# Turning normalised tiles by DMA, as two 16-bit planes, in the memory attention of a six-block kernel

## The chip, the cores and the metric

The kernel runs on one core of a Trainium2 chip. The metric is the device time of one execution in microseconds (us); the kernel before took 2589.55 us, the median of 3 runs (2587.43 to 2590.55). Work is spread over TensorE (PE in the profile), VectorE (DVE), ScalarE (ACT), GpSimd (POOL), and transfers whose instructions are queued on SyncE (SP).

## The reference

The program runs six residual blocks over eight sequences of 1024 tokens with 256 features, all in fp32: an FP4 feed-forward, a decaying linear attention, the same FP4 feed-forward, a ternary feed-forward, a memory attention, and the ternary feed-forward again. The change lies in the memory attention. Cut to what matters, that block is:

```python
x = layernorm(x)
q, k, v = x @ wq.T, x @ wk.T, x @ wv.T          # 16 heads of 16
sq, sk = elu(q) + 1, elu(k) + 1
out_m = sq @ memories[m] / (sq . memory_norms[m])     # 4 memories
mem_out = sum over m of softmax_m(mean of sq . memory_norms[m]) * out_m
local = (sq @ cumsum(sk v^T)) / (sq . cumsum(sk))     # causal linear attention
x = x + (g * mem_out + (1 - g) * local) @ w_o.T
```

## The kernel before

The 8192 tokens are 64 tiles of 128 tokens, held on the 128 partitions, and 16 groups of 4 tiles; a sequence is 2 groups. TensorE contracts over partitions, so each normalised tile, tokens by features, has to be turned to features by tokens before it can be multiplied by the projection weights. The turned group is the tile `xt`, 2 halves of 128 features by 512 tokens.

The block is `attn_memory`. A prelude at step 0 normalises, turns and projects groups 0 to 2. Then a loop runs 64 steps and 5 more that drain it; step i works on tile i, which is tile j = i mod 4 of its group, and on older tiles in later stages. A group is projected (line 2003: q or k, 512 tokens at a time, one half of the features a step) in the steps j = 3, 0, 1, 2, two to three groups ahead of its own attention. Tile keys and values come from `keys` (line 1745), which reads `xt` again at the group's own steps. In each step:

- TensorE computes scores (`sc`, line 1263), products with the memories (`pmo`, 1786), the weighted values (`py`, 1329 and 1347), the transpose `psd` (1929), in a step with j = 3 the divisors (`pr`, 1667), the transposes `pyt` and `pn` (1969, 1973), a projection (`pk` or `pq`, 1361), the output product `po`, in a step with j = 2 the turning of a group, and the keys and values `pkv` (1754, 1361).
- VectorE first runs the batch statistics of later tiles that are due in that step (`ln.advance(i, 0)`, line 1951), then the reciprocal `rw` (1955), `y` (1981), two of the four score weightings (`at`, 1272), the layer-norm terms that are due (`ln.advance(i, 1)`, line 1998), the last `at`, the output addition (2014), the elu (1627), and the weightings of the next step's memory products (1799). In every second step a running sum (1646) stands ahead of the statistics.
- ScalarE copies results out of PSUM (`nt` 1914, `yt` 1976, `vz` 1763, `kd` 1770), computes `ee` (1622, 1623), masks queries (`qz`, 1774) and normalises groups (`norm`, two instructions a tile, lines 317 and 325).
- GpSimd adds the memories (1902), adds `y` (1989), the state (1944), the clamps (1680) and the products by the running sum (1636).

`norm(t + 1)` is written in a step with j = 1, `norm_turn(t + 1, (3, 0))` in the next one, with t = i // 4 + 2. `norm_turn` makes eight 128x128 transposes on TensorE into two PSUM banks and copies each bank to `xt` on ScalarE. There is one buffer for the normalised group `xn`, and four for `xt`.

Two things set the order. Whatever goes through `pin` (all of TensorE and VectorE here) keeps the order of the program text. ScalarE and GpSimd are not pinned in this block: the framework's planner places their instructions, the earliest in the text first among those that it takes to be ready, so an instruction far down in the text can be moved forward into a gap. SP has nothing queued in this block.

The statistics of later groups are spread over the steps by `PLANS["memory"]`: sizes of the shares in groups, and for each the step by which it is due. A share has a statistics entry for each tile (`bn_stats` and `bn_aggr`, lines 235 and 236) and four entries of layer-norm terms at its end (a seed of three instructions, lines 248 to 255, and three Newton steps of three, lines 262 to 264), all on VectorE.

Of the kernel before, what the change touches and what calls it, by code (L numbers as in the profile page):

```python
# [9 lines left out]
F32 = mybir.dt.float32  # L10
F32R = mybir.dt.float32r
BF16 = mybir.dt.bfloat16
I32 = mybir.dt.int32
AF = mybir.ActivationFunctionType
ALU = mybir.AluOpType
AX = mybir.AxisListType
# [2 lines left out]
P = 128  # L19
D = 256  # L20
# [3 lines left out]
G = 4  # L24
TG = G * P
# [14 lines left out]
def macaron_kernel(  # L40
# [25 lines left out]
    nc = tc.nc  # L66
    NB, S, _ = x.shape
    NG = NB * S // TG
    GB = S // TG
# [60 lines left out]
    for g in range(NG):  # L130
        xg = xpool.tile([P, G, D], F32, name=f"x_{g}")
        X.append(xg)
        if g == 0:
# [4 lines left out]
                out=A0.lng[:, H : H + 2], in_=gamma_rep.rearrange("(m p) -> p m", p=P)  # L138
# [23 lines left out]
    for m in range(NM):  # L162
        nc.sync.dma_start(
            out=mem_d[:, :, m, :],
            in_=memories[m].rearrange("h d e -> (h d) e").rearrange("(c p) e -> p c e", p=P),
        )
        nc.sync.dma_start(
            out=nrm_d[:, :, m],
            in_=memory_norms[m].rearrange("h d -> (h d)").rearrange("(c p) -> p c", p=P),
# [10 lines left out]
        out=tri, in_=ones, pattern=[[1, P]], compare_op=ALU.is_ge, fill=0.0, base=0,  # L180
# [5 lines left out]
        out=blk8, in_=ones[:, 0:HT], pattern=[[-HD, HT]], compare_op=ALU.is_ge, fill=0.0, base=0,  # L186
# [3 lines left out]
        out=blk8, in_=blk8, pattern=[[HD, HT]], compare_op=ALU.is_ge, fill=0.0, base=HD - 1,  # L190
# [47 lines left out]
    def norm_terms(mv, r, b):  # L238
# [8 lines left out]
        def seed():  # L247
# [3 lines left out]
                nc.vector.tensor_scalar(  # L251
                    r.bitcast(I32), va.bitcast(I32), -0.5, float(RSQRT_SEED), ALU.mult, ALU.add
                )
# [14 lines left out]
    def statistics(sizes, dues):  # L268
# [44 lines left out]
        def normalize(dst, g, only=None, pin=lambda ins: ins, apart=False):  # L313
            def centred(j):
                n = G * g + j
                pin(
                    nc.scalar.activation(
                        dst[:, j, :], X[g][:, j, :], AF.Identity, bias=lb[:, n : n + 1]
                    )
                )  # L320

            def scaled(j):
                n = G * g + j
                pin(
                    nc.scalar.activation(
                        dst[:, j, :], dst[:, j, :], AF.Copy, scale=lr[:, n : n + 1]
                    )
# [25 lines left out]
        "ternary": ((2, 2, 4, 4, 4), [max(0, g - 1) for g in range(NG)]),  # L353

        "memory": (
            (GB + 3, 3, 4, NG), [max(0, G * (g - GB) - 4) for g in range(NG)]
        ),
    }
    begun = {}
# [1 line left out]
    def begin(kind, left):  # L361

        if kind not in begun:
            ln = statistics(*PLANS[kind])
            begun[kind] = [ln, list(ln.first)]
        ln, shares = begun[kind]
        for _ in range(-(-len(shares) // left)):
            shares.pop(0)()
        if left == 1:
            xn = xn_pool.tile([P, G, D], F32, tag="xn", name="xn")  # L370
            ln.normalize(xn, 0)
            begun[kind] = (ln, xn)
# [16 lines left out]
    def fp4_round(v, sc, pool, mul, pin):  # L389
        vb = v.rearrange("p (b k) -> p b k", k=16)  # L390
        np_, nb, _ = vb.shape
        mg = pool.tile([P, nb * 16], F32, tag="q_mg", name="q_mg")[:np_]
        nc.scalar.activation(mg, v, AF.Abs, scale=FP4_MAGIC)

# [4 lines left out]
    def transpose_group(src, dst, psum, tag, both_act=False, pin=lambda ins: ins):  # L399

        for k in range(2):
            pt = psum.tile([P, TG], F32, tag=tag, name="pt")
            for j in range(G):
                pin(
                    nc.tensor.transpose(
                        pt[:, j * P : (j + 1) * P], src[:, j, k * P : (k + 1) * P], ident
                    )
                )
            if k == 0 or both_act:
                nc.scalar.copy(dst[:, k, :], pt)  # L410
            else:
                pin(nc.vector.tensor_copy(dst[:, k, :], pt))

    def fp4_first(xn, mg, pool):

        v = xn.rearrange("p t d -> p (t d)")
        vb = v.rearrange("p (b k) -> p b k", k=16)
        nb = G * D // 16
        wide = [P, nb, 16]
        am = pool.tile([P, nb], F32, tag="q0_am", name="q_am")  # L420
        pin(nc.vector.tensor_reduce(am, vb, AX.X, ALU.max, apply_absolute_value=True))
        sc = pool.tile([P, nb], F32, tag="q0_sc", name="q_sc")
        pin(nc.vector.tensor_scalar(sc, am, -1.0 / 6.0, -1e-12, ALU.mult, ALU.min))
        rs = pool.tile([P, nb], F32, tag="q0_rs", name="q_rs")
        pin(nc.vector.tensor_scalar(rs, sc, -FP4_TIE, None, ALU.mult))
        pin(nc.vector.reciprocal(rs, rs))
        nc.gpsimd.tensor_tensor(vb, vb, rs[:, :, None].to_broadcast(wide), ALU.mult)

        def magnitudes():
            nc.scalar.activation(mg, v, AF.Abs, scale=FP4_MAGIC)  # L430

        def round_it():
            for op in (ALU.add, ALU.subtract):
                pin(nc.vector.scalar_tensor_tensor(v, mg, FP4_LEAST, v, ALU.max, op))
            nc.gpsimd.tensor_tensor(vb, vb, sc[:, :, None].to_broadcast(wide), ALU.mult)

        return magnitudes, round_it
# [10 lines left out]
    with (  # L448
# [16 lines left out]
        def log_decays():  # L465
            pin(nc.scalar.activation(gsig, gsig, AF.Sigmoid))

            pin(nc.scalar.activation(ea, A0.lng, AF.Abs))
            pin(nc.scalar.activation(ea, ea, AF.Exp, scale=-1.0))
            pin(nc.scalar.activation(ea, ea, AF.Ln, bias=1.0))  # L470

        ii = prep_q.tile([P, P], I32, name="ii", bufs=1)
        df = prep_q.tile([P, P], F32, name="df", bufs=1)
        nc.gpsimd.iota(ii, pattern=[[1, P]], base=0, channel_multiplier=-1)
        nc.gpsimd.tensor_copy(df, ii)
        nc.gpsimd.tensor_scalar(df, df, 0.0, 1.0, ALU.max, ALU.mult)
        ii2 = prep_q.tile([P, P], I32, name="ii2", bufs=1)
        tf = prep_q.tile([P, P], F32, name="tf", bufs=1)
        nc.gpsimd.iota(ii2, pattern=[[1, P]], base=1, channel_multiplier=0)
        nc.gpsimd.tensor_copy(tf, ii2)  # L480
        ii3 = prep_q.tile([P, 1], I32, name="ii3", bufs=1)
        sf = prep_q.tile([P, 1], F32, name="sf", bufs=1)
# [107 lines left out]
        xn = xn_pool.tile([P, G, D], F32, tag="xn", name="xn")  # L590
# [776 lines left out]
    def attn_decay(after):  # L1367
        with ExitStack() as st:
# [18 lines left out]
            def norm_turn(g):  # L1387
                xt = lnp.tile([P, 2, TG], F32, tag="xt", name="xt")
                transpose_group(xns.pop(g), xt, ps_b, "pb", both_act=True, pin=pin)
                qz = lnp.tile([P, 2, 2, TG], F32, tag="qz", name="qz")  # L1390
                qg = lnp.tile([P, 2, TG], F32, tag="qg", name="qg")
                kt = lnp.tile([P, 2, TG], F32, tag="kt", name="kt")
                proj[g] = (xt, qz, qg, kt)
# [175 lines left out]
    def attn_memory(after):  # L1569
        with ExitStack() as st:  # L1570
            lnp = st.enter_context(tc.tile_pool(name="a1_ln", bufs=2))
            bp = st.enter_context(tc.tile_pool(name="a1_b", bufs=GB + 2))
# [4 lines left out]
            ps_s = st.enter_context(tc.tile_pool(name="a1_ps", bufs=4, space=PSUM))  # L1577

            ps_n = st.enter_context(tc.tile_pool(name="a1_pn", bufs=1, space=PSUM))
            xns, proj, sums, mix, state, chunk, ys = {}, {}, {}, {}, {}, {}, {}  # L1580
            ksum, carry = {}, {}
            vzs = spaced_values(vp)
# [4 lines left out]
            def bank(n, shape, name):  # L1587
                return ps_n.tile(shape, F32, tag=f"b{n}", name=name)

            def norm(g):  # L1590
                xn = xn_pool.tile([P, G, D], F32, tag="xn", name="xn")
                ln.normalize(xn, g)
                xns[g] = xn

            def norm_turn(g, banks, both_act=True):
                xt = bp.tile([P, 2, TG], F32, tag="xt", name="xt")
                xn = xns.pop(g)
                for k in range(2):
                    pt = bank(banks[k], [P, TG], "pt")
                    for j in range(G):  # L1600
                        pin(
                            nc.tensor.transpose(
                                pt[:, j * P : (j + 1) * P], xn[:, j, k * P : (k + 1) * P], ident
                            )
                        )
                    if k == 0 or both_act:
                        nc.scalar.copy(xt[:, k, :], pt)
                    else:
                        pin(nc.vector.tensor_copy(xt[:, k, :], pt))
                sq = bp.tile([P, 2, TG], F32, tag="sq", name="sq")  # L1610
                sk = bp.tile([P, 2, TG], F32, tag="sk", name="sk")
                proj[g] = (xt, sq, sk)
# [194 lines left out]
            n = NG * G  # L1807
            clamps, summed = [], None
            held = {}
            for i in range(n + 5):  # L1810
                a, b, c, d, e = i - 1, i - 2, i - 3, i - 4, i - 5
                g, j = divmod(i, G)
                t = g + GB
# [187 lines left out]
                if i < n and last < NG:  # L2001
                    m, of_q = (j + 1) % 4 // 2, j % 2 == 0
# [19 lines left out]
                weigh_one(0)  # L2022
                if added:
                    added()
                if i < n and j == 2 and t + 1 < NG:
                    norm_turn(t + 1, (3, 0))
                if i < n:
                    keys(i, 3 if elu else 2)
# [11 lines left out]
                    output()()  # L2040
                if i < n and i % CB == 0:
                    mixing[2]()
                if i < n and j == 1 and t + 1 < NG:
                    norm(t + 1)
                if n - 14 <= i < n - 2:
                    begin(after, n - 2 - i)

# [6 lines left out]
    f0_stack.close()  # L2054
    ffn_ternary(False, "memory")
    attn_memory("ternary")
    ffn_ternary(True)

# [47 lines left out]
```

## Time and profile before

| | |
|---|---|
| median of 3 runs | 2589.55 us |
| the profiled execution | 2594.43 us, of which the span from first to last instruction is 2592.7 |
| memory attention (first `pt` transpose to last `psd`) | 1749 to 2315 us |
| PE busy in it, 1990 to 2060 us | 69.48 of 70 us |
| DVE, ACT, POOL there | 60.95, 40.48, 39.12 of 70 us |
| transposes of `xn` (line 1602) in the block | 128, of which 104 in the loop |
| copies of them on ScalarE (line 1607) | 29, mean 588 ns |

A busy TensorE is not at its peak, since its instructions overlap and their ends are modelled; the chain of work that ended last tells better how much time each of them holds up the rest. A duration of an instruction in the groups (273 ns for a transpose) is longer than its share of the chain for the same reason. In the timeline, the bracket behind an instruction is the idle time of its engine before it and what ended it.

### The profile page before, as it was taken

The page shows a single profiled execution, that of the slowest core. Times are in us where ns is not written, and L with a number is a line of the kernel's source. Part 1 is how long each engine was busy: PE and PEld are TensorE (multiplying, and loading weights), DVE is VectorE, ACT ScalarE, POOL GpSimd, SP SyncE. Part 2 cuts the span into 40 slices and gives each one's busy share as a digit, 9 for nine tenths or more (in the row PEclk, how much of TensorE's full clock was granted, in tenths as well). Part 3 has the DMA queues.
Part 4 walks back from the last instruction along what each step waited for, and adds up shares of the span by engine and source line. Part 5 has one row for each costly group of instructions (what it writes and reads, how often), then busy time and mean ns, then how long its engine had stood idle before and what let it go on. Part 6 is the DMA issues. An engine that isn't in the chain of part 4 may idle for free.

```text
span 2592.7 us, 52415 instructions
## 1 busy us (share of the span) xinstructions
PE 2506.9 (97%) x20426; PEld 1868.6 (72%) x20426; DVE 2087.8 (81%) x4808; ACT 1235.1 (48%) x2785; POOL 900.9 (35%) x895
## 2 busy tenths in 40 slices
PE   4899999999999999999999999999999999999999
PEld 2577777766666666777777689995677776778998
DVE  7898888758878778988888599647888888879864
ACT  5344444334333333444444276656555555437664
POOL 4565555521101003555555300004555555530000
PEclk9899999999999999999999999999999999999999
DMA  7455556500000002556555300000000000000001
GB/s 218 87 117 115 113 118 116 107 23 18 10 22 14 2 2 48 114 116 115 117 116 113 66 1 1 1 1 1 2 2 2 2 2 2 2 2 26 33 33 41
DMA packets 199897, 132.40 MB, mean 51 GB/s; under 512 B 138048, under 2 KB 174944, under 8 KB 199648
## 3 DMA queue, kind: packets, MB, share of 16 engines
q1 hardware_dynamic: 198704, 127.85, 22.8%
q8 instruction: 161, 2.64, 0.4%
q0 software_dynamic: 240, 0.54, 0.1%
q14 instruction: 88, 0.72, 0.1%
q10 hardware_dynamic: 704, 0.66, 0.1%
HBM read 80.77 MB, written 16.52 MB: 38 GB/s over the span
## 4 chain that ended last, share of the span: by engine, by line
PE 84%; DVE 11%; ACT 2%; issue 1%; DMA 1%; POOL 1%; SPq 0%; DVEq 0%; POOLq 0%; ACTq 0%
PE po L960 11%; PE pu L861 10%; PE pg L861 10%; PE po L1220 9%; PE ph L1193 9%; PE sc L1263 5%; PE py L1347 5%; PE pq L1361 4%; PE pkv L1361 4%; PE po L1361 4%; PE pk L1361 4%; PE py L1329 2%; PE pmo L1786 2%; DVE at L1272 1%; DVE qp L804 1%
## 5 line engine op out<-in xcount | busy, mean ns | idle before, releaser
L960 PE MATMUL po<-wd,ht 128*128 128x256 f32 x1536 | 358.1, 383 | 0.6 <-DVE x L969 0.5
L861 PE MATMUL pu<-wgu,xt 128*128 128x352 f32 x1024 | 349.6, 464 | 8.3 <-DVE h L876 7.9
L861 PE MATMUL pg<-wgu,xt 128*128 128x352 f32 x1024 | 348.8, 463 | 4.4 <-ACT sg L871 4.1
L960 PEld LDWEIGHTS po<-wd,ht 128*128 128x128 f32 x1536 | 294.6, 193 | 62.4 <-issue 2.2
L871 ACT ACTIVATE sg<-pg 128x352 f32<-128x352 f32 x256 | 118.1, 461 | 451.5 <-PE pg L861 422.6
L817 POOL TENSOR_TENSOR h<-h,q_rs 128x704 f32<-128x704 f32 (+1 forms) x128 | 176.2, 1376 | 413.1 <-DVE q_rs L811 413.1
L861 PEld LDWEIGHTS pu<-wgu,xt 128*128 128x128 f32 x1024 | 186.5, 193 | 112.3 <-issue 19.6
L861 PEld LDWEIGHTS pg<-wgu,xt 128*128 128x128 f32 x1024 | 195.0, 191 | 97.8 <-ACT sg L871 9.2
L1220 PE MATMUL po<-w,hl 128*128 128x256 f32 x1024 | 243.7, 280 | 1.4 <-DVE hl L1204 1.2
L1220 PE MATMUL po<-w,hh 128*128 128x256 f32 x1024 | 243.3, 280 | 0.0
L1902 POOL TENSOR_TENSOR mo<-mo 128x256 f32<-128x256 f32 x192 | 164.2, 855 | 196.6 <-DVE mo L1799 188.1
L927 POOL TENSOR_TENSOR ht<-gt,ht 128x768 f32<-128x768 bf16 x124 | 205.7, 1659 | 0.0
L1193 PE MATMUL ph<-xh,w 128*128 128x512 f32 x512 | 204.4, 401 | 1.4 <-ACT hf L1201 0.6
L1193 PE MATMUL ph<-xl,w 128*128 128x512 f32 x512 | 201.8, 395 | 0.0
L1204 DVE TENSOR_TENSOR hl<-hf,hh 128x512 fp32r<-128x512 f32 x256 | 168.3, 684 | 39.4 <-ACT hh L1202 35.9
L1220 PEld LDWEIGHTS po<-w,hl 128*128 128x128 f32 x1024 | 192.1, 188 | 4.5 <-DVE hl L1204 2.5
L1220 PEld LDWEIGHTS po<-w,hh 128*128 128x128 f32 x1024 | 192.1, 188 | 2.6 <-DVE x L1228 0.3
L1201 ACT ACTIVATE hf<-ph,b1c 128x512 f32<-128x512 f32 x256 | 168.0, 695 | 18.5 <-PE ph L1193 16.1
L1272 DVE TENSOR_TENSOR at<-sc,dec 128x512 f32<-128x512 f32 x256 | 158.6, 682 | 11.8 <-PE sc L1263 11.8
L886 DVE SCALAR_TENSOR_TENSOR h<-qp,h 128x704 f32<-128x704 f32 x124 | 110.2, 889 | 69.1 <-ACT qp L821 68.9
L1272 DVE TENSOR_TENSOR at<-sc,tri 128x512 f32<-128x512 f32 x256 | 164.9, 679 | 0.4 <-PE sc L1263 0.4
L1202 ACT CAST hh<-hf 128x512 fp32r<-128x512 f32 x256 | 149.2, 628 | 17.0 <-PE po L1220 15.2
(276 smaller groups left out, 5303.0 us busy)
## 6 DMA issues: line engine op xcount, KB each, us to landing
ht<-sd SPq DMA_DIRECT2D x124, 384.0 KB
xt<-sd SPq DMA_DIRECT2D x56, 256.0 KB
sd<-sct SPq DMA_DIRECT2D x124, 64.0 KB
x<-in_x SPq DMA_DIRECT2D x15, 512.0 KB
out<-x SPq DMA_DIRECT2D x15, 512.0 KB
t_raw<-in_w_t SPq DMA_DIRECT2D x16, 256.0 KB
gt<-gd SPq DMA_TRANSPOSE x124
gtx<-xn SPq DMA_TRANSPOSE x56
```

The costliest lines, as they stand in the source:

```text
L817: pin(mul.tensor_tensor(vb, vb, rs[:, :, None].to_broadcast([P, nb, 16]), ALU.mult))
L861: nc.tensor.matmul(ps, lhsT=xts[g][:, 2 * j + k, :], rhs=wgu[:, k, (2 * q + of_up) * NHALF : (2 * q + of_up + 1) * NHALF], start=(k == 0), ...
L927: nc.gpsimd.tensor_tensor(wide.rearrange("p c t -> p (c t)"), grid.rearrange("p c t -> p (c t)"), wide.rearrange("p c t -> p (c t)"), ALU. ...
L960: nc.tensor.matmul(po, lhsT=ht[:kn, c, :], rhs=wd[:kn, c, :], start=(c == 0), stop=(c == NC - 1),)
L1193: nc.tensor.matmul(ph, lhsT=w1[:, k, f * P : (f + 1) * P], rhs=xt[:, k, :], start=(k == 0 and xt is xh), stop=(k == 1 and xt is xl),)
L1201: nc.scalar.activation(hf, ph, AF.Gelu, bias=b1c[:, f : f + 1])
L1202: nc.scalar.copy(hh[:, f, :], hf)
L1204: nc.vector.tensor_tensor(hl[:, f, :], hf, hh[:, f, :].bitcast(F32), ALU.subtract)
L1220: nc.tensor.matmul(po, lhsT=ht[:, f, j * P : (j + 1) * P], rhs=w2[:, f, :], start=(f == 0 and ht is hh), stop=(f == NF - 1 and ht is hl),)
L1272: nc.vector.tensor_tensor(at, sc.rearrange("p m (e t) -> p (m e) t", e=2), weight, ALU.mult)
L1361: nc.tensor.matmul(dst, lhsT=lhsT, rhs=rhs, start=n == 0, stop=n == len(parts) - 1)
L1902: summed = nc.gpsimd.tensor_tensor(mo[:, :, :, 0, :], mo[:, :, :, 0, :], mo[:, :, :, m, :], ALU.add)
```

## The change

Groups 0 to 3 are turned as before. From group 4 on, and so for 12 groups, each tile is turned by itself. At the end of a step, GpSimd takes the tile apart into its low and high 16-bit halves (`apart`, two planes of 256), and one DMA transpose on SP's queue turns both planes, four blocks of 128x128 (`turned`). At the end of the next step ScalarE joins the halves into the tile's columns of `xt`. Both new tiles have one buffer. The tiles are taken in the steps j = 2, 3, 0, 1; the last is joined in a step with j = 2, before the projection of the group in j = 3.

`norm` for these groups comes a group earlier: `norm(t + 2)` at the end of the step with j = 1, behind the taking apart of the last tile of the group before, whose `xn` buffer it uses. The plan of the statistics has shares of 5, 2, 2, 3 and 4 groups instead of 5, 3, 4 and 4, due by steps 0, 5, 13, 21 and 33 instead of 0, 8, 20 and 36. The transposes into PSUM and their copies fall away for the 12 groups.

```diff
         "memory": (
-            (GB + 3, 3, 4, NG), [max(0, G * (g - GB) - 4) for g in range(NG)]
+            (GB + 3, 2, 2, 3, NG), [max(0, G * (g - GB) - 7) for g in range(NG)]
         ),
...
+    def planes_turned(xj, pool, copy):
+
+        apart = pool.tile([P, 2, D], U16, tag="apart", name="apart")
+        copy(apart, xj.bitcast(U16).rearrange("p (n b) -> p b n", b=2))
+        turned = pool.tile([P, 4, P], U16, tag="turned", name="turned")
+        nc.sync.dma_start_transpose(out=turned, in_=apart.rearrange("p b n -> p (b n)"))
+        return turned
+
+    def planes_joined(turned, xt, j, copy):
+        words = xt[:, :, j * P : (j + 1) * P].bitcast(U16)
+        copy(
+            words.rearrange("p k (t b) -> p b k t", b=2),
+            turned.rearrange("p (b k) t -> p b k t", b=2),
+        )
...
+            gp = st.enter_context(tc.tile_pool(name="a1_g", bufs=1))
+            turning, xts = {}, {}
...
             def norm_turn(g, banks, both_act=True):
-                xt = bp.tile([P, 2, TG], F32, tag="xt", name="xt")
-                xn = xns.pop(g)
-                for k in range(2):
+                xt = xts.pop(g, None)
+                xn = xns.pop(g, None)
+                if banks:
+                    xt = bp.tile([P, 2, TG], F32, tag="xt", name="xt")
+                for k in range(2) if banks else ():
...
-                if i < n and j == 2 and t + 1 < NG:
+                if i < n and j == 2 and t + 1 < NG and i < G:
                     norm_turn(t + 1, (3, 0))
...
-                if i < n and j == 1 and t + 1 < NG:
+                if i < n and j == 1 and t + 1 < NG and i < G:
                     norm(t + 1)
+                for m, v in list(turning):
+                    turned = turning.pop((m, v))
+                    if v == 0:
+                        xts[m] = bp.tile([P, 2, TG], F32, tag="xt", name="xt")
+                    planes_joined(turned, xts[m], v, nc.scalar.copy)
+                    if v == G - 1:
+                        norm_turn(m, None)
+                if i == 2 and t + 2 < NG:
+                    norm(t + 2)
+                v = (j - 2) % G
+                m = t + 2 if j > 1 else t + 1
+                if 1 < i < n and m < NG:
+                    xj = xns[m][:, v, :]
+                    turning[m, v] = planes_turned(xj, gp, nc.gpsimd.tensor_copy)
+                if G < i < n and j == 1 and t + 2 < NG:
+                    norm(t + 2)
```

More of the change, by code (lines that the diff above doesn't have):

```diff
@@ L13 @@
 I32 = mybir.dt.int32
+U16 = mybir.dt.uint16
 AF = mybir.ActivationFunctionType
```

## The prediction

> **What bounds the kernel now.** I read the engine shares and slices on the page first, then the busy time by stretches of the memory attention, then the chain of work that ended last, and last the timelines of VectorE and ScalarE.
>
> ```profile
> PE 2506.9 (97%) x20426; PEld 1868.6 (72%) x20426; DVE 2087.8 (81%) x4808; ACT 1235.1 (48%) x2785; POOL 900.9 (35%) x895
> ...
> ACT  5344444334333333444444276656555555437664
> POOL 4565555521101003555555300004555555530000
> ...
> DMA  7455556500000002556555300000000000000001
> ```
>
> The block fills slices 27 to 36. ScalarE and GpSimd are half idle there, and the DMA engines wholly.
>
> ```profile
> 1990.00:2060.00 70.00, 69.48 (x994) 49.62 (x983) 60.95 (x144) 40.48 (x105) 39.12 (x54) 1.00 0.01 2
> ```
>
> The columns are the stretch, its length, then busy time of PE, weight loads, DVE, ACT and POOL. PE fills 69.48 of 70 us at the full granted clock, DVE 60.95. So PE bounds the block, with DVE close behind.
>
> The chain around one turning (start, length, what), from the `psd` transpose of one step to that of the next:
>
> ```profile
> 2033.04 0.23 PE psd L1929
> ...
> 2036.43 0.45 PE pt L1602 x4
> 2036.88 0.02 issue
> 2036.90 0.59 ACT xt L1607
> 2037.49 0.05 issue
> 2037.54 0.44 PE pkv L1754 x2
> ...
> 2043.90 0.23 PE psd L1929
> ```
>
> I measure steps from `psd` to `psd`. This one takes 10.86 us; the other steps of a plain group take 7.69, 7.82 and 7.81. Two things make it longer, the turning and the divisors `pr`. The last group, which has no turning, goes from 2241.07 to 2250.60 by the timeline: with `pr` alone, 9.53 us. The difference, 1.33 us, agrees with the rows above: 1.11 from the first `pt` to `pkv`, and `pkv` at 0.44 instead of the 0.22 it takes elsewhere.
>
> DVE, a step in which layer-norm terms are due (lines 262 to 264):
>
> ```profile
> 1942.00 1.28 DVE L1272 TENSOR_TENSOR at<-sc,tri 128x512 f32<-128x512 f32 x2
> ...
> 1943.71 0.65 DVE L264 SCALAR_TENSOR_TENSOR ln_r<-ln_h,ln_r 128x16 f32<-128x16 f32 x1
> ...
> 1944.91 0.68 DVE L1272 TENSOR_TENSOR at<-sc,tri 128x512 f32<-128x512 f32 x1
> ```
>
> Two Newton steps stand between the third and the fourth `at`, 1.78 us, and that step took 9.40 us against 7.69: nearly all of it was lost. The reason is a second chain: PE's `psd` and `pn` release `rw`, and from the end of the last `at` to the next `py` on line 1347 it is 2.34 to 2.60 us in every step without a turning. That leaves 0.0 (j = 3), 0.16 (j = 0) and 0.26 us (j = 1) of slack. Only the step with j = 2 has more, 1.48 us, because PE is turning there.
>
> **The change part by part.**
>
> Removed from PE: 12 groups at 1.33 us, 16.0 us. This is what the chain can give if nothing else comes late. With it the slack of VectorE in the steps j = 2 falls from 1.48 to 0.15 us.
>
> New plan of the statistics, terms. Each share's four entries come last, so their steps follow from the plan. Before: seed or Newton steps in i = 6, 7, 18, 19, 33, 34, 35. Those in 6, 18 and 34 (j = 2) hid behind the turning; those in 7, 19, 35 (two Newton steps, j = 3) cost 1.5, 1.71 and 1.71 us, the seed in 33 0.72: in all 5.6. After, one share more, and none behind a turning: seed in 3 (0.98, which is 0.72 and the slack), three Newton steps in 4 (1.78 and 0.6 for the third, less 0.16: 2.2), seed in 10 (0.83), one Newton step in 11 (1.1), two in 12, 20 and 32 (1.62 each), seed and one in 19 and 31 (1.7 each). That is 13.4; the first two steps I take at half, since the output additions have not begun by then: 11.8. So 6.2 us more. Bounds: 0, if VectorE catches up, and 9 with the first two in full and the 0.95 us seed of line 248 each time.
>
> Statistics entries. Two in a step cost nothing where VectorE waits before `rw` (j = 1 and 3: 0.83 and 2.33 us), and 0.49, 0.63 and 0.77 us in steps 10, 12 and 16 of before, where it doesn't: 1.9 us. The last plan before had its double steps at j = 3 only. After, the double steps with j = 0 or 2 are 6, 8, 14, 16, 18, 22, 26, 28: eight at 0.55, 4.4 us. So 2.5 us more; bounds 0 and 4.
>
> GpSimd: 48 copies of 512 16-bit elements. No row shows them. From a 128x128 conversion (289 ns) and a 128x1 copy (198 ns) follow 0.57 us; the two-input product of 512 elements (1281 ns) is the other end. I take 0.6, nearest to the single-input rows. GpSimd is idle 31 of 70 us, in pieces of up to 4.2 us before line 1902. Without that cover it is the product `kc` (1636) that would come late for the divisors, which has 2.65 us to spare. Cost nothing; a copy of 1.3 us still fits.
>
> DMA: 48 transposes on SP's queue, which has nothing else in the block, so none is passed. One from the FP4 stage, and the GB/s from 1448.4 us on in slices of 0.1 us:
>
> ```profile
> 1449.02 1.24 SPq L912 DMA_TRANSPOSE gt<-gd  x1
> ...
> GB/s 31 0 0 0 15 133 205 226 72 5 0 0 0 0 0 0 0 0 77 202 207 207 233 210 210 202 213 162 44 0 0 0 0 184 215 154 215 184 215 215
> ```
>
> The six blocks flow from 1450.2 to 1451.3: 1.2 us after issue, for 1.05 us. Four blocks take 0.7. So copy, transfer and join make some 0.6 + 1.9 + 0.6, 3.2 us with the hand-overs, in a step of 7.8 us. The worst row is a transpose behind a 384 KB transfer, waited for until 4.84 us after issue; 6.1 us would still fit. With one buffer of each, the next transfer waits for the join before; that leaves a step for each tile. The turned group is wanted at j = 3, a step after its last issue. Cost nothing.
>
> A rule speaks against this: the Trainium skill, VectorE: DVE Perf Modes, section "The three transpose paths", gives 390 ns for a 128x128 bf16 transpose on TensorE and 1309 ns by DMA, and advises TensorE when PSUM will do. By its figure, as an estimate, a tile's four blocks take 5.2 us and the round 6.4, still inside the step, so the sum would be the same; here TensorE's own price is the 0.11 us that a transpose holds up the chain.
>
> ScalarE: 24 copies of 588 ns go, 48 joins of 512 elements come. Nearest row: the SBUF to SBUF cast of 128x512, 628 ns; bounds 0.59 and, for the unseen 16-bit strided form, twice that, 1.26. Written at a step's end they stand here:
>
> ```profile
> 2015.60 0.91 ACT L1774 ACTIVATE qz<-sq,pm 128x256 f32<-128x256 f32 x2 [0.86 <-PE pmo L1786]
> 2017.35 0.37 ACT L1914 COPY nt<-py 128x256 f32<-128x256 f32 x1 [0.84 <-PE py L1347]
> ```
>
> A gap of 0.84 us covers 0.63. Behind the join are queued `nt`, which PE's `pn` waits for with 0.1 us to spare, then the state, `yt` and `ee`. The eight instructions of a `norm` (0.45 apart, 3.6 us) ran right behind the `xt` copies at j = 2, and `nt` came late there, but `pr` covered it. Now they follow the last taking apart, in j = 1 or 2, where `pr` does not cover `nt`. I charge half an instruction, 0.2 us, for each of 12 groups: 2.5 us. Bounds: a gain of 2.7 (the 2.7 us that PE's loads waited for `xn` go away) and a loss of 20, 48 joins at 0.42 over the gap.
>
> Sum: -16.0 + 6.2 + 2.5 + 2.5 = -4.8 us, -0.19%. The profiled execution would go from 2594.43 to 2589.6; it lay 4.9 us above the median, and the same difference on the median gives 2584.8.
>
> **The rivals.**
>
> *VectorE catches up.* If the terms spill into the waits before `rw` in the steps j = 1 and 3, both plan items fall to about 1 us: -16 + 1 + 1 + 1, some 2576.5. For it: DVE is busy only 87%. Against: 1.71 of 1.78 lost before.
>
> *ScalarE becomes the wait (slower).* A join that takes over 0.84 us, or that the planner sets ahead of `ee` before the transfer has landed, holds `nt` or `ee`, and through them `pn` or the elu. At 1.26 us it costs 20: 2589.55 - 4.8 + 20 = 2605. It decides from 0.2 us a tile: 48 x 0.2 is 10, and the time is 0.2% over before. For it: the planner's order can't be read from the trace of before. Against: ScalarE is idle 3.9 us in a plain step.
>
> *The step j = 2 does not shrink,* because the moved `norm` fills what the turning leaves. Then the plan items stay alone: some 2598. Against: the copies, 1.2 us a group, leave ScalarE in that very step.
>
> **How the numbers follow.** A change under 0.2%, 5.2 us, can't be told from none here. The forecast, a gain mostly eaten by VectorE (2578 to 2590), has 50 in 100, about half of it beyond 0.2%; VectorE catching up 12; ScalarE as the wait 28, a fifth of it within 0.2%; the step that does not shrink 10. Faster: 25 + 12 = 37. Same: 25 + 5 = 30. Slower: 23 + 10 = 33. The range 2574 to 2605 runs from nearly the whole 16 us to a join of twice the row.
>
> **What would show it.** Line 1602 at 32 transposes and line 1607 at 5 copies on ScalarE; plain groups after step 36 at 32.9 instead of 34.2 us; steps after i = 4, 12, 20 and 32 longer by 1.6 or more; joins near 0.63 us; no wait of ScalarE for the DMA. Wrong if joins take over 0.84 us, if `pn` waits for `nt` in most steps, or if steps with terms are no longer than plain ones.

## The result and the profile after

The changed kernel takes 2660.8 us (median of 4 runs, 2658.35 to 2662.32) against 2590.05 us before on the same chip: a ratio of 1.0274, with a 95% interval of 1.0256 to 1.0292. The profiled executions are 2658.35 us (span 2656.6) and 2594.43 us. The change makes the kernel 71 us slower, where 5 us faster was predicted, and the time lies outside the range of 2574 to 2605.

The page of the kernel after: engine shares, and the slices of ScalarE, GpSimd and the transfers.

```profile
PE 2518.4 (95%) x20330; PEld 1870.0 (70%) x20330; DVE 2090.9 (79%) x4820; ACT 1254.9 (47%) x2809; POOL 924.5 (35%) x943
...
ACT  5344444343333324444443466655555554436665
POOL 4556555420100004555554100025545555540000
...
DMA  7455555400000004555555000000000000000101
```

No engine has much more to do than before: ScalarE has 19.8 us more, GpSimd 23.6, VectorE 3.1, and TensorE has 96 matmuls fewer. What is lost is waiting. The same 70 us of the memory attention (the stretch, its length, then busy time and count of PE, weight loads, DVE, ACT and POOL, the granted clock, and the share and GB/s of the transfers):

```profile
1990.00:2060.00 70.00, 59.46 (x776) 40.31 (x769) 52.23 (x126) 35.96 (x89) 37.35 (x55) 0.93 0.07 15
```

TensorE is busy 59.5 us of 70 where it was busy 69.5, with 776 matmuls where there were 994, and its granted clock is 0.93 instead of 1.00. Every other engine is less busy too: all stand behind something for a part of the time.

Steps are measured from `psd` to `psd`, as in the prediction, and named by the j of the `psd` that they begin with. The step that turned did get shorter. The chain of work through a step with j = 2 (start, length, what), from one `psd` to the next:

```profile
2153.43 0.23 PE psd L1949
...
2155.95 0.86 PE po L1377 x4
2156.82 0.22 PE pkv L1774 x2
...
2161.24 1.71 PE pr L1687 x12
2162.95 0.23 PE psd L1949
```

It takes 9.52 us instead of 10.86: `po` goes straight into `pkv`, and nothing is turned between them. The loss is in the step j = 0, once in each of the 12 groups that are turned by DMA. Here is the chain through one of them:

```profile
2047.77 0.88 PE pkv L1377 x4
2048.67 0.37 ACT vz L1783
2049.04 0.28 ACT kd L1790
2049.32 0.67 ACT xt L425
...
2050.04 2.41 DMA turned<-apart
...
2052.51 0.61 POOL apart L418
...
2053.31 2.42 DMA turned<-apart
...
2055.75 0.77 ACT xt L425
2056.52 0.48 ACT xn L318
2057.00 0.27 ACT nt L1934
...
2057.32 0.44 PE pn L1993 x2
2057.75 3.37 PE pq L1377 x4
```

The path that sets the end now runs through ScalarE's join (line 425), a transfer, GpSimd's taking apart, another transfer, another join and `norm` (line 318) before it reaches `nt`, which `pn` needs. ScalarE's timeline at the same place (start, length, instruction; in brackets the idle time before it and what ended it) shows why:

```profile
2048.94 0.38 ACT L1790 COPY kd<-pkv 128x256 f32<-128x256 f32 x1
2049.20 0.78 ACT L425 COPY xt<-turned 128x512 uint16<-128x512 uint16 x1
2052.48 0.77 ACT L425 COPY xt<-turned 128x512 uint16<-128x512 uint16 x1 [2.50 <-DMA turned<-apart]
2053.11 0.90 ACT L1794 ACTIVATE qz<-sq,pm 128x256 f32<-128x256 f32 x2
2055.75 0.77 ACT L425 COPY xt<-turned 128x512 uint16<-128x512 uint16 x1 [1.75 <-DMA turned<-apart]
2056.49 0.51 ACT L318 ACTIVATE xn<-x,ln_b 128x256 f32<-128x256 f32 x1
2056.91 0.35 ACT L1934 COPY nt<-py 128x256 f32<-128x256 f32 x1
```

The text writes one join at the end of each step. The planner has put three of them, and the start of `norm`, into one place, ahead of `nt`. Since `apart` and `turned` have one buffer each, the second join can't run before the first has freed `turned`, and a transfer has been made after it; the third needs another such round; and `norm` needs the last taking apart, whose `xn` buffer it overwrites. So ScalarE, which runs its instructions in their order, stands still for 2.50 and 1.75 us with `nt` behind it. The chain of waits from 1800 to 2380 us (who waited on which line, for what; us in total, times, longest):

```profile
POOL apart L418 <- DMA turned<-apart: 104.7, 36, 7.5
...
PEld pn L1993 <- ACT nt L1934: 64.3, 38, 5.9
ACT xt L425 <- DMA turned<-apart: 58.1, 26, 3.1
PE pn L1993 <- ACT nt L1934: 57.1, 14, 5.7
```

TensorE waited 57.1 us for `nt` at line 1993; before, it waited 0.4 us for `nt` in the same stretch. Its weight loads waited 64.3 us there; before, they waited 5.9 us.

Step lengths make the account. The means of four plain groups late in the loop (steps 36 to 51):

| us | j = 0 | j = 1 | j = 2 | j = 3 | group |
|---|---|---|---|---|---|
| before | 8.13 | 7.53 | 10.86 | 7.63 | 34.15 |
| after | 14.99 | 7.53 | 9.53 | 7.63 | 39.68 |

The turning gives 1.33 us a group, as foreseen, and the step j = 0 takes 6.86. Over the 12 groups these steps are 78.0 us longer than before.

### The profile page after: what moved, and what is told of

Its sections match the earlier page's. It is cut to its first block, busy times and chain, and to the rows that moved or that the text cites. A ratio compares the mean times of both kernels' runs of the same rounds, so it can differ in the third digit from the quotient of the medians.

```text
span 2656.6 us, 52415 instructions
## 1 busy us (share of the span) xinstructions
PE 2518.4 (95%) x20330; PEld 1870.0 (70%) x20330; DVE 2090.9 (79%) x4820; ACT 1254.9 (47%) x2809; POOL 924.5 (35%) x943
## 3 DMA queue, kind: packets, MB, share of 16 engines
q1 hardware_dynamic: 224816, 134.14, 23.6%
## 4 chain that ended last, share of the span: by engine, by line
PE 82%; DVE 10%; ACT 3%; DMA 2%; issue 2%; POOL 1%; ACTq 0%; DVEq 0%; POOLq 0%; SPq 0%
PE po L976 11%; PE pu L877 10%; PE pg L877 10%; PE po L1236 9%; PE ph L1209 8%; PE pq L1377 4%; PE sc L1279 4%; PE py L1363 4%; PE po L1377 4%; PE pk L1377 4%; PE pkv L1377 4%; PE py L1345 2%; DMA turned<-apart 2%; PE pmo L1806 1%; DVE at L1288 1%
## 5 line engine op out<-in xcount | busy, mean ns | idle before, releaser
L1922 POOL TENSOR_TENSOR mo<-mo 128x256 f32<-128x256 f32 x192 | 154.9, 807 | 108.0 <-DVE mo L1819 100.4
L1288 DVE TENSOR_TENSOR at<-sc,dec 128x512 f32<-128x512 f32 x256 | 158.6, 683 | 11.8 <-PE sc L1279 11.8
```

Source lines behind the costliest of these rows:

```text
L1288: nc.vector.tensor_tensor(at, sc.rearrange("p m (e t) -> p (m e) t", e=2), weight, ALU.mult)
L1922: summed = nc.gpsimd.tensor_tensor(mo[:, :, :, 0, :], mo[:, :, :, 0, :], mo[:, :, :, m, :], ALU.add)
```

## The experiments

Two theories stood against each other first. A: the joins, which the planner crowds together, wait for the transfers, and hold `nt`. B: ScalarE simply has more to do than fits. C, beside them, is the new plan of the statistics on VectorE.

### Joins held to their steps

```diff
-                nc.scalar.copy(                      # vz
+                keyed["last"] = nc.scalar.copy(
...
-                    nc.scalar.copy(kd, pkv[:, 0, :])
+                    keyed["last"] = nc.scalar.copy(kd, pkv[:, 0, :])
...
-                    planes_joined(turned, xts[m], v, nc.scalar.copy)
+                    with tc.issue_after(keyed["last"].ins):
+                        planes_joined(turned, xts[m], v, nc.scalar.copy)
```

The planner may not set a join ahead of the last copy of the step's keys.

> Theory A: the 70 us are ScalarE standing in order behind joins whose transfer has not landed, because the planner moved three joins of a group forward into one step, ahead of `nt`. Here a join may not be issued before the last copy of `keys` of the step it is written in, so there is one a step and each transfer has most of a step. A expects ScalarE's waits for the DMA (58 us) to fall below 3 us, and 2595 to 2612 us in all: the eight instructions of a `norm` now stand together ahead of one `nt` and make it 1 to 2 us late in each of 12 groups. Theory B, ScalarE simply has too much to do (48 joins of 0.77 us): no change, 2650 or more. Theory C, the new plan of the statistics on VectorE: no change, 2650 or more.

Measured: 2651.18 us, a ratio of 1.0234 (1.0218 to 1.0249). Only some 10 us come back. The joins no longer wait for any transfer, and yet the stall is there, one step later. TensorE's wait for `nt`, from 1800 to 2380 us, and ScalarE of this kernel:

```profile
PE pn L1993 <- ACT nt L1934: 44.3, 13, 5.5
```

```profile
2054.55 0.38 ACT L1790 COPY kd<-pkv 128x256 f32<-128x256 f32 x1
2054.82 0.77 ACT L425 COPY xt<-turned 128x512 uint16<-128x512 uint16 x1
2059.69 0.91 ACT L318 ACTIVATE xn<-x,ln_b 128x256 f32<-128x256 f32 x2 [4.10 <-POOL apart L418]
2060.50 0.89 ACT L326 ACTIVATE xn<-xn,ln_r 128x256 f32<-128x256 f32 x2
...
2062.89 0.35 ACT L1934 COPY nt<-py 128x256 f32<-128x256 f32 x1
```

Now the whole of `norm`, eight instructions, stands ahead of `nt`. It waits 4.10 us for the last taking apart, then runs for 3.2 us. The late steps j = 0 are back at 8.18 us, and the steps j = 1 take 12.1 to 15.2 in 11 groups, where 7.53 was plain. Theory A falls as it was put: the joins alone are not the cause. By its time alone, this run lies where B and C put it. Theory A is widened to A2: whatever the planner sets ahead of `nt` while it has to wait for the round of one buffer holds TensorE, and a join or a `norm` is enough for it.

### The plan of the statistics alone

```diff
 # the kernel before, turned by TensorE as it was
-            (GB + 3, 3, 4, NG), [max(0, G * (g - GB) - 4) for g in range(NG)]
+            (GB + 3, 2, 2, 3, NG), [max(0, G * (g - GB) - 7) for g in range(NG)]
```

> The kernel before with the new plan of the statistics and nothing else of the change. Theory C expects most of the 70 us: 2640 or more. Theories A and B expect 2592 to 2599 us: the terms in steps 4, 11, 12, 19, 20, 31 and 32 make these steps longer by 1 to 2 us each, the ones of steps 7, 19, 33 and 35 before are gone.

Measured: 2595.63 us, 1.0019 (1.0010 to 1.0028): the plan costs the kernel before 4.7 us. Theory C can't explain 71; A and B had 2592 to 2599 us here.

### No transfer

```diff
-        turned = pool.tile([P, 4, P], U16, tag="turned", name="turned")
-        nc.sync.dma_start_transpose(out=turned, in_=apart.rearrange("p b n -> p (b n)"))
-        return turned
+        return apart.rearrange("p b (k t) -> p (b k) t", k=2)
```

> The changed kernel without the 48 DMA transposes: the join reads the planes as GpSimd left them, so the tiles of groups 4 to 15 are not turned and the projections work on unturned data. Everything else is issued as before, the joins crowded as before. Theory A expects no wait for a DMA and most of the loss gone, 2590 to 2615 us; theory B, the load of ScalarE being the same, 2645 to 2660.

Measured: 2650.77 us, 1.0237 (1.0222 to 1.0252). Groups 4 to 15 are joined without having been turned, and all 48 transfers are gone; that gives back 10 us of 71. ScalarE of this kernel, at the place of the stall:

```profile
2045.63 0.79 ACT L423 COPY xt<-apart 128x512 uint16<-128x512 uint16 x1 [0.70 <-POOL apart L418]
2048.00 0.76 ACT L423 COPY xt<-apart 128x512 uint16<-128x512 uint16 x1 [1.59 <-POOL apart L418]
...
2049.47 0.91 ACT L318 ACTIVATE xn<-x,ln_b 128x256 f32<-128x256 f32 x2
...
2051.88 0.35 ACT L1932 COPY nt<-py 128x256 f32<-128x256 f32 x1
```

The joins wait less, 0.70 and 1.59 us, and now more of `norm` comes ahead of `nt`, which is still late: TensorE waits 50.2 us for it from 1800 to 2380 us. Theory A missed with its 2590 to 2615 us, and the time is again where B put it. The transfer as such is not the cause: without any, joins that wait for the taking apart, and `norm`, still stand ahead of `nt`.

### Joins and norm held to their steps

`norm` is cut into its four tiles. Tile `part` is normalised behind `yt` of the same step in which it will be taken apart, into one group-sized tile `xn_all` that stays. The joins are held as above.

```diff
+                part = (j - 2) % G
+                to = t + 2 if j > 1 else t + 1
+                ahead = 1 < i < n and to < NG
...
-                    nc.scalar.copy(yt, pyt)
+                    copied = nc.scalar.copy(yt, pyt)
...
+                    if ahead:
+                        with tc.issue_after(copied.ins):
+                            ln.normalize(xn_all, to, part)
...
-                if i == 2 and t + 2 < NG:
-                    norm(t + 2)
...
-                if G < i < n and j == 1 and t + 2 < NG:
-                    norm(t + 2)
```

> As the run with one join a step, and the two normalising instructions of one tile in each step as well, behind `yt`, where ScalarE is idle for 1.5 us, instead of eight together. Theory A expects all of the loss gone and what the prediction had without its ScalarE item: -16 for the turning, +6 to +9 for the plan of the statistics, 2580 to 2590 us. Theory B expects 2640 or more.

Measured: 2586.89 us, 0.9983 (0.9973 to 0.9992). With the same 48 joins, 48 copies, 48 transfers and as many normalisations, 74 us are gone, and plain groups take 8.13, 7.54, 9.53 and 7.63 us, in all 32.83, against the predicted 32.9. TensorE's wait for `nt` in the same stretch is gone:

```profile
PE pn L1996 <- ACT nt L1934: 0.4, 2, 0.2
```

Theory B falls: ScalarE's load, which is the same, was not the trouble.

### Norm held, joins free

The same kernel without the two lines that hold the joins.

> Theory A fell in its first form: without any transfer 60 of the 70 us stayed, and so they did with one join a step. New form, A2: what costs is whatever the planner sets ahead of `nt` on ScalarE while it waits on the one-buffer round (take apart, transfer, join, and a `norm` whose buffer the last taking apart frees); joins alone and `norm` alone are each enough. This run has the normalising instructions tile by tile behind `yt`, and the joins left to the planner, which sets two of them together once a group. A2 expects one wait for a transfer a group, 2 to 3 us late each: 2605 to 2630 us. Rival A3, the `norm` is all of it and joins are harmless: 2583 to 2592, as with both held. Rival A4, the joins are all of it: 2640 or more.

Measured: 2604.96 us, 1.0054 (1.0040 to 1.0068), at the lower edge of what A2 expected and outside what both rivals did. The waits of this kernel:

```profile
ACT xt L425 <- DMA turned<-apart: 40.9, 22, 3.0
...
PE pn L1996 <- ACT nt L1934: 15.5, 12, 1.9
```

This completes a table of four kernels, all with the turning by DMA (us):

| | `norm` free | `norm` held |
|---|---|---|
| joins free | 2660.8 | 2605.0 |
| joins held | 2651.2 | 2586.9 |

Free joins alone cost 18 us, the free `norm` alone 64, both 74. They don't add up. A likely reason, which no run shows by itself, is that with both free the two waits fall into one stall: the changed kernel loses time in the steps j = 0, and its late steps j = 1, where the free `norm` alone cost most, keep their 7.53 us.

### Norm as a whole, one step later

The joins held, and the eight instructions of `norm` together as the change has them, but in the step with j = 2 behind `yt`, when the last tile has been taken apart:

```diff
-                if G < i < n and j == 1 and t + 2 < NG:
-                    norm(t + 2)
...
+                    if G < i < n and j == 2 and t + 2 < NG:
+                        with tc.issue_after(copied.ins):
+                            norm(t + 2)
```

> One join a step, as in the first run, and the eight instructions of `norm` still together, but behind `yt` of the step j = 2, a step after the last taking apart of the group before, so that they need not wait for it and do not stand ahead of `nt`. If the loss with the joins held (60 us) is the wait for that taking apart and the place ahead of `nt` (A2), it goes but for the 2.1 us by which 3.6 us overfill a gap of 1.5: 2590 to 2610 us. If eight of them together cost wherever they stand, 2640 or more.

Measured: 2591.43 us, 1.0001 (0.9991 to 1.0011). So it was not the cutting of `norm` that cured the kernel. Moving it behind `nt`, and behind what it waits for, gives back 60 of the 64 us. The remaining 4.5 lie mostly in the steps j = 2, where the eight instructions now stand: from step 34 to 46 they take 10.50 us instead of 9.53.

### The place alone, in the kernel before

No join, no transfer, nothing that waits for either: in the kernel before, `norm(t + 1)` of groups 4 to 15 is put ahead of `nt`.

```diff
-                if i < n and j == 1 and t + 1 < NG:
+                if 1 < i < n and j == 0 and t + 1 < NG:
+                    with tc.issue_after(keyed["last"].ins):
+                        norm(t + 1)
+                elif i == 1:
                     norm(t + 1)
```

> The kernel before, turned by TensorE, with the eight instructions of `norm` held behind `kd` of a step j = 0, so that they stand ahead of `nt` of the step j = 1 and wait for nothing. It prices the place alone: 3.6 us of `norm` and 0.9 of `qz` where 2.6 us are free, `nt` 1.5 to 2 us late in each of 13 groups. A2 expects 2608 to 2618 us. If only waits cost and the place does not: 2588 to 2594.

Measured: 2603.24 us, 1.0048 (1.0034 to 1.0062): 12.2 us for the 12 groups, less than the 2608 to 2618 us that A2 expected and more than the rival's 2588 to 2594. The late steps j = 1 take 8.87 us instead of 7.53. The wait of TensorE:

```profile
PE pn L1973 <- ACT nt L1914: 13.5, 13, 1.3
```

Eight instructions of ScalarE in front of `nt`, with their data ready, cost 1.0 us a group. It is a cost that the prediction had put at 0.2, but it is not the 5 us a group that the free `norm` alone cost in the table: that kernel has the wait of up to 4.2 us for the last taking apart as well, and behind it the slower clock that the last section shows.

### The statistics put into VectorE's wait

In the kernel with joins and `norm` held, VectorE still waits long ahead of the `rw` that the text has at j = 3, while TensorE makes `pr`:

```profile
1937.57 0.66 DVE L1975 RECIPROCAL rw<-psd 128x80 f32<-128x80 f32 x1 [3.49 <-ACT state L1959]
```

Here each share's seed and three Newton steps are put ahead of one such `rw`, and the entries into steps that have room:

```diff
+            shares = [s for u in sorted(ln.plan) for s in ln.plan[u]]
+            ln.plan.clear()
+            for ends, places in (
+                (3, ((0, 2), (1, 3), (2, 3))),
+                (11, ((4, 1), (5, 2), (7, 4), (8, 1))),
...
+            ):
+                for u, size in places + ((ends, 4),):
+                    ln.plan.setdefault(u, []).extend(shares[:size])
+                    del shares[:size]
...
-                    ln.advance(i, 0)
+                    ln.advance(i)
...
-                if i < n:
-                    ln.advance(i, 1)
```

> One join and one tile's `norm` a step, and the statistics placed by hand: all terms of a share in a step j = 3, ahead of `rw`, where VectorE waits for `pr` (2.3 to 3.4 us), and entries of the tiles only where it waits, none in a step j = 2. If the prediction's reading of VectorE's slack is right, the steps up to 36 become as long as those behind it (9.53, 7.5, 7.8 to 8.45, 7.8): the kernel with one join and one tile's `norm` a step loses some 12 us, 2570 to 2578. If VectorE had caught up anyway, no change: 2584 to 2590.

Measured: 2568.62 us, 0.9912 (0.9899 to 0.9926). It is faster than the kernel before and the changed one. VectorE at the same place:

```profile
1933.31 0.17 DVE L265 SCALAR_TENSOR_TENSOR ln_r<-ln_h,ln_r 128x12 f32<-128x12 f32 x1
1933.40 0.65 DVE L1987 RECIPROCAL rw<-psd 128x80 f32<-128x80 f32 x1
```

The twelve term instructions end where the wait was, and `rw` follows without a pause. The same 70 us by stretches:

```profile
1990.00:2060.00 70.00, 69.97 (x944) 49.69 (x944) 65.37 (x152) 47.35 (x114) 47.30 (x69) 1.00 0.10 17
```

TensorE is busy all the time, at the full granted clock, and nearly every step has the length of a plain one.

The same placing in the kernel before, which turns on TensorE, with the same sizes of the shares, tells the turning from the statistics:

> The kernel before, turned by TensorE, with the statistics placed as in the run with terms in the wait. It tells what of that run's gain is owed to the turning by DMA. From the steps over their plain length before (1.5, 0.5, 0.6, 0.8, 1.7, 0.7 and 1.7 us): 2579 to 2586; the difference to the turning by DMA should then be 8 to 16 us.

Measured: 2584.41 us, 0.9971 (0.9961 to 0.9981). Between these two kernels, which share the statistics and differ in how tiles are turned (and so in when they are normalised), lie 15.8 us; in the two profiled executions 15.2 of them are in the steps j = 2. That is the worth of turning by DMA here, when nothing else comes late.

## Why the prediction was wrong

**What failed.** Two sentences of it. Of the transfers: "With one buffer of each, the next transfer waits for the join before; that leaves a step for each tile … Cost nothing." Of ScalarE: "I charge half an instruction, 0.2 us, for each of 12 groups: 2.5 us." Both priced joins and `norm` where the text writes them, spread over the steps. The planner set two or three joins and part of `norm` together, and then the one buffer no longer leaves a step for each tile: it makes a chain of copy, transfer and join, 3.3 us from one join to the next, and the chain stood ahead of `nt`. With both held in their steps 74 us went away, 6.2 a group, where 0.2 had been charged. That it is these two placements, and neither the transfers as such, nor ScalarE's load, nor the plan, is shown by the runs. Why the planner places them so is not: the costs that it assumes are not to be seen in a trace, and no run varied them. More buffers for `apart` and `turned` were not tried.

**The rival that named it.** "ScalarE becomes the wait" had a join "that the planner sets ahead of `ee` before the transfer has landed". That is the mechanism, with `nt` in place of `ee`, and it was given 28 in 100. Its price, 20 us, was worked out for joins that are too long (0.42 us over a gap, 48 times), not for joins that wait for a transfer. A join that waits holds `nt` for a round or two, less the gap of 0.84: by the prediction's own 3.2 us, 12 groups with two rounds come, as an estimate made afterwards, to (6.4 - 0.84) x 12, some 67 us. That end was missing from the range. And `norm`, named as a term, had no rival of its own, though the change makes it wait for a taking apart where before its data had long been ready.

**Its marks.** Line 1622 (1602 before) has 32 transposes and line 1627 five copies, as foreseen. Plain groups take 39.7 us instead of 32.9. ScalarE waits 58.1 us for the transfers, where no wait was foreseen, and `pn` waits for `nt` in one step of each group. That is fewer than the "most steps" named as the sign of being wrong, and it was enough; the joins, at 0.767 us, stayed under the 0.84 named as another. Of the other rivals, the step j = 2 did shrink, and VectorE did not catch up by itself; it took the entries and terms only where they were put into its waits by hand.

**What held, and what was only mis-sized:**

- Turning: 16.0 us were worked out from 10.86 against 9.53; the late steps measured 9.52 or 9.53, and the pair of kernels 15.8.
- GpSimd's copy: 0.610 us in the median, estimated 0.6. The two rows of the instructions (shortest, median and longest in ns, first and last start, shape):

```profile
L418 POOL COPY apart<-xn x48: 608/610/1542, 1795.5 to 2255.3; 128x512 uint16<-128x512 uint16 x48
...
L425 ACT COPY xt<-turned x48: 751/767/797, 1802.2 to 2258.5; 128x512 uint16<-128x512 uint16 x48
```

- The join: 0.767 us in the median, estimated 0.63. It is still inside the gap of 0.84, and in the kernel with both held `nt` is not late.
- The round: worked out as 3.2 us, measured as 4.0 from the start of the copy to the end of the join (0.61, 2.42 and 0.77 with the hand-overs). It still fits in a step.
- Layer-norm terms after the change: 11.8 us were worked out. Between the kernel with joins and `norm` held and the one with the statistics moved, the steps that the prediction lists (3, 4, 10, 11, 12, 19, 20, 31 and 32) differ by 13.3 us, 1.1 of them in step 10, which has a statistics entry as well. Step 4 cost more than thought (3.5 for 2.2, which was then taken at half), steps 12, 20 and 32 less (1.3 for 1.6).
- Statistics entries after the change: 4.4 us were worked out. In the same pair the eight double steps differ by 6.4: 0.65 to 0.77 us in 6, 8, 14, 16, 22 and 28, and 1.10 in 18 and 26, for 0.55. The single entry in step 30 cost 0.66 us (10.19 for 9.53), where nothing had been charged. TensorE no longer turns in a step with j = 2, and the slack of 0.15 us that the prediction itself gave for these steps is less than such an entry.
- The plan before: 7.5 us were worked out, and moving its statistics gave 6.6. The prediction put the terms of steps 7 and 33 at 1.5 and 0.72 us; they measure 1.69 and 1.28.

Moving the statistics gave 18.3 us in the changed kernel with joins and `norm` held, and 6.6 in the kernel before, so the plan cost 11.7 us more instead of 8.7. (The steps listed come to 20.4 and the two profiled executions differ by 20.0 us in the loop; the medians of the runs differ by 18.3.)

With both held in their steps the kernel was 4.0 us faster than before, and the prediction had 4.8. That it comes so near is luck: the plan cost 3.0 us more than worked out, and the 2.5 us charged to ScalarE were not paid. No run left `norm` at the very place where the text writes it, so what the sum is worth for a ScalarE in the order of the text is not shown.

## What to carry to other kernels

A price worked out for an instruction where the text writes it holds only if its place is pinned; where a planner orders an engine, ask of each new instruction what it waits for, and what could be queued behind it if it were placed as early as its text order allows, and put that in the range. One buffer for a round over three engines is harmless while its uses lie a step apart and a chain as soon as two of them are put side by side. Work that waits long can be held behind what must be in time with one dependency; and fixed small work belongs in the waits of its own engine, not beside its busiest stretch.

## What the runs showed of the hardware

The stall costs more than its length, because TensorE comes out of it at half its clock. PE's timeline after a stall in the changed kernel, and the stretch behind it (the third figure from the end is the granted clock):

```profile
2057.32 0.44 PE L1993 MATMUL pn<-ident,nt 128*128 128x128 f32 x2 [4.88 <-ACT nt L1934]
2057.59 3.53 PE L1377 MATMUL pq<-xt,wq 128*128 128x512 f32 x4
...
2057.68:2061.09 3.41, 3.41 (x6) 1.35 (x5) 3.00 (x6) 2.21 (x7) 1.87 (x4) 0.50 0.20 38
```

and the same after a short one in the kernel with `norm` held and the joins free:

```profile
2025.11 0.44 PE L1996 MATMUL pn<-ident,nt 128*128 128x128 f32 x2 [1.89 <-ACT nt L1934]
2025.38 1.88 PE L1377 MATMUL pq<-xt,wq 128*128 128x512 f32 x4
...
2025.38:2027.26 1.88, 1.88 (x7) 0.92 (x6) 1.77 (x5) 1.22 (x4) 1.01 (x4) 1.00 0.00 0
```

The same four matmuls take 3.53 us instead of 1.88, at a granted clock of 0.50 instead of 1.00. Over five kernels, between 1830 and 2250 us: after an idle time of up to 1.9 us they took 1.88 us in 19 of 20 cases; after 2.5 to 3.4 us, 1.88 to 3.54 us in eight; after 4.3 us and more, 3.03 to 3.62 us in all 22. In the changed kernel the ten that were seen have a mean of 3.40. That makes 1.5 us a group, and, as an estimate for 12 groups, some 18 us of the 78.0 that are lost in the steps j = 0 would be the clock and not the wait. The Trainium skill, TensorE: Matmul & The Clock Gate, section "Why this matters for your kernels", advises no idle gaps over about 3 us between bursts of matmuls, since the clock then falls to half; the rows agree in the long stalls, and those between 2.5 and 3.4 us are mixed. They show no sharp limit: the one exception among the short ones, an idle time of 1.90 us in the kernel with `norm` held and the joins free, was followed by 3.23 us at a granted clock of 0.56.

The DMA transpose of a tile's four 16-bit blocks landed 2.41 us after its issue in the chain. The estimate that the prediction drew from the Trainium skill, VectorE: DVE Perf Modes, section "The three transpose paths", was 5.2 us. That page's advice to transpose on TensorE when PSUM will do (section "Rules for kernel authors") does not hold in this block: with TensorE busy 69.48 of 70 us and the DMA engines idle, turning fp32 tiles as two 16-bit planes by DMA was worth 15.8 us.
